# Moving three queries' additions, the output weights' loads and the first output pair's small work in a one-core decoder layer

## The chip, the cores and the metric

The kernel runs on one core of a Trainium2 chip. Its time is the device time of one execution in microseconds, taken as the median of several runs. All stages described below run on that core: TensorE (PE) multiplies, VectorE (DVE), ScalarE (ACT) and GpSimd (POOL) do the elementwise work, and transfers are issued by SyncE (SP) or by ACT, each on a queue of its own.

## What is computed

The input is `x` of 32 sequences of 64 tokens with 512 numbers each, that is 2048 tokens, all in float32. Three blocks follow each other, each added to its input:

```
x = x + attention(layernorm(x))      # 32 heads of 128, rmsnorm on q and k, softmax over 64 keys, @ Wo + bo
x = x + cross(layernorm(x), ctx)     # keys and values from a context of 64 x 128 per sequence, plus a skip product
x = x + experts(layernorm(x))        # softmax of 64 logits, top 8, weighted expert biases
```

Most of the arithmetic is in the first: q, k and v are products of 2048 x 512 by 512 x 4096 each, and the output is 2048 x 4096 by 4096 x 512.

## The kernel before

The tokens are 16 tiles of 128, and two halves of 8 tiles are worked one after the other. For each half a loop runs over 16 head groups of two heads (`hg`). A head group's q and k products are done by a fast matrix scheme with 7 products in place of 8, and from the second head group on by that scheme twice over: a `Window` holds both quads of tiles of the half (two units, t = 0 and 1) and computes 7 x 7 products. So there are 15 windows in each half, 30 in all.

A window's `project` has four outer stages, n = 0 to 3. Stage n hands `outer` two of the seven outer products, (1, 5), (2, 6), (7, 3), and in the last stage (4,) alone. `outer` stops several times (m = 0 to 3). PE's products go to three PSUM banks `pa`, `pb`, `pc`; `keep` (L670, or L673 on ACT) writes a bank into the `qk` tile with an addition, and `end` (L683) adds a bank to what is there. A bank that PE adds to again (`first=False`) waits until DVE has read it. In stage 3 the order is: product 1 in `pa`, product 2 in `pc`, their two reads, stop (3, 0); product 6 in `pa`, product 5 in `pb`, two reads, stop (3, 1); products 7 and 3, two reads, stop (3, 2); product 4, its read, stop (3, 3).

At each stop the work that `behind` names for (n, m) is issued first: `add` (L739) sums quarters of `qk` tiles on DVE for the second unit and on POOL for the first, and `squares` (L360) squares a tile on ACT for the rms norm. Then follow waiting operations and what `plan[n][m]` lists: a value product `v` (L391 on PE, L407 copies on ACT, L411 adds on DVE), the scaling of an earlier unit (`scale`: k on POOL L546 at once, q on DVE L548 at a later `take_waiting`), the turning of probabilities (`turn`: L253 on PE, L582 on ACT), and attention of an earlier unit (`attend`: scores L559, mixing L596, softmax L261 to L269). At the end of the window `sums_of_squares` (L792) multiplies the squares by ones on PE. Meanwhile POOL forms the next window's weight sums (L120, L152 to L155) into a buffer that SP's loads (L107) filled. In the last window of a half POOL has no such inner sums (L152 to L155) to form. `also(n, m, it)` adds a step to a stop.

The order on PE, DVE, ACT and POOL is the order of the program up to the end of the first output pair; SP's order is left to the planner of the language. An engine's stream is executed in order, and an instruction that waits holds what is behind it. This is true of the transfers that ACT and SP issue, too.

Before the last window `load_wo` (L823) loads the output weights: eight transfers of 1 MB in all, k for the head of a pair, n for the half of the columns. They reuse the two large buffers of the weights (`four_blocks`) and the seven blocks of the transposed input (`block`).

After the last window comes the output product. `first_out` works the first pair of tiles: seven products (1, 2, 3, 7, 6, 5, 4) of 16 matmuls, each cut in four chunks. `drain` steps through its 28 chunks with `go(count)`, and puts the last units' `scale`, `turn` and `attend` between them. After chunk number `done`, DVE does what `sums[done]` holds (L902: sums of the first pair's inputs) or the next of eight sums of output weights (`making_wo`, L874 and L882) at chunks 8, 10, 14, 15, 16, 18, 21, 22. Then `strassen_out` does the other seven pairs, while `advance` moves the tails (cross attention and experts) of finished tiles. Ahead of the tails a small product `wqk` of the cross attention's weights is made from `xw` (L1510 to L1536). The chunks of the second pair are drawn by `next(outs[1])`.

Of the kernel before, what the change touches and what calls it, by code (L numbers as in the profile page):

```python
# [41 lines left out]
def decoder_layer(  # L42
# [585 lines left out]
    class Window:  # L628
# [86 lines left out]
        def project(self, plan):  # L715

            units, hg = self.units, self.w.hg
            for unit in units:
                unit.qk_tiles()
            sq = self.sq = {}  # L720

            def of(places):
                return lambda t, j: units[t].all[:, places, j, :]

            def twice(place):
                return lambda t, j: (
                    units[t].all[:, place, j, :].unsqueeze(1).to_broadcast([P, 2, QT])
                )

            def squares(h, ab, t):  # L730
                sq[h, ab, t] = square(
                    units[t].qk[h, ab], f"{h}{ab}_{units[t].name}", ab
                )

            def add(t, j, to, what):

                to, what = (units[t].qk[it][:, j, :] for it in (to, what))
                on = nc.vector if t else nc.gpsimd
                on.tensor_tensor(to, to, what, ALU.add)  # L739


            behind = {
                (1, 3): lambda: [squares(0, 0, t) for t in range(2)],
                (2, 1): lambda: (
                    add(0, 0, (1, 0), (1, 1)),
                    add(0, 0, (1, 1), (0, 1)),
                ),
                (2, 2): lambda: (
                    add(0, 1, (1, 0), (1, 1)),
                    add(0, 1, (1, 1), (0, 1)),  # L750
                    add(1, 1, (1, 0), (1, 1)),
                ),
                (2, 3): lambda: (
                    add(1, 1, (1, 1), (0, 1)),
                    add(1, 0, (1, 0), (1, 1)),
                    squares(1, 0, 0),
                    squares(1, 1, 0),
                ),
                (3, 0): lambda: (
                    add(1, 0, (1, 1), (0, 1)),  # L760
                    squares(1, 0, 1),
                ),
                (3, 1): lambda: squares(1, 1, 1),
                (3, 2): lambda: squares(0, 1, 0),
                (3, 3): lambda: squares(0, 1, 1),
            }
            for n, args in enumerate(
                (
                    ((1, 5), of(slice(2, 4)), None, lambda j: bqd[:, j, bass.ts(hg, HG)]),
                    ((2, 6), of(slice(0, 3, 2)), twice(2)),  # L770
                    ((7, 3), of(slice(1, 3)), twice(2)),
                    ((4,), of(slice(1, 2)), of(slice(1, 2))),
                )
            ):

                banks = [self.bank(f"p{n}{i}") for i in range(3)]
                turned = [banks[(2 * n + i) % 3] for i in range(3)]
                for m, _ in enumerate(self.outer(args[0], turned, *args[1:])):
                    behind.get((n, m), lambda: None)()
                    take_waiting()  # L780
                    for it in plan[n][m]:
                        it()
# [31 lines left out]

    def load_wo(k, n, places):


        halves = []  # L820
        for i, it in enumerate(places):
            it = it.rearrange("p (g f) -> p g f", f=DH)
            nc.scalar.dma_start(  # L823
                out=it,
                in_=wo.rearrange("(g k p) f -> k p g f", k=HG, p=HD)[
                    k, :, i * KH : (i + 1) * KH, bass.ts(n, DH)
                ],
            )
            halves.append(it)
        return halves  # L830
# [63 lines left out]
    def first_out(a, right, s4, s1, done):  # L894


        (a11, a12), (a21, a22) = a
        xa, xb = load_x(0), load_x(1)
        la, ra, lb, rb_ = (xt[:, bass.ts(n, DH)] for xt in (xa, xb) for n in range(2))
        p1 = xpool.tile([P, D], F32, tag="x", name="p1_0")[:, 0:DH]  # L900
        def combine(op, to, x, y):
            return lambda: nc.vector.tensor_tensor(to, x, y, op)  # L902

        sums[3] = combine(ALU.add, s1, a21, a22)
        sums[4] = combine(ALU.subtract, a11, s1, a11)
        sums[5] = combine(ALU.subtract, s4, a12, a11)
        sums[7] = combine(ALU.subtract, a21, a22, a11)

        def product(i, it):
            py = out_block(f"{i}_0")  # L910
            yield from chunks(py, [(it, right[i])])
            return py

        def add(to, py):
            nc.vector.tensor_tensor(to, to, py, ALU.add)

        py = yield from product(1, a11)
        nc.scalar.copy(p1, py)
        yield
        py = yield from product(2, a12)  # L920
        add(la, py)
        nc.gpsimd.tensor_tensor(la, la, p1, ALU.add)
        yield
        py = yield from product(3, s4)
        add(ra, py)
        yield
        py = yield from product(7, a21)
        add(lb, py)
        add(rb_, py)
        yield  # L930
        py = yield from product(6, a11)
        add(p1, py)
        for to in (ra, lb, rb_):
            nc.gpsimd.tensor_tensor(to, to, p1, ALU.add)
        yield
        py = yield from product(5, s1)
        add(ra, py)
        add(rb_, py)
        add_bias(xa)
        done(0, xa)  # L940
        yield
        py = yield from product(4, a22)
        add(lb, py)
        add_bias(xb)
        done(1, xb)
# [396 lines left out]
    for n, (hg, half) in enumerate(groups):  # L1342
# [37 lines left out]
        else:  # L1380
# [34 lines left out]

            if n + 1 == len(groups):
                four = four_blocks("wo_0")
                wo_b = [[load_wo(k, 0, four[2 * k : 2 * k + 2])] for k in range(2)]
                a_0 = [[None, None], [None, None]]

                def mixture(t, h, place):
                    a_0[t][h] = load_mixed(t, h, place())

                def qk_buffer(name):
                    return work.tile([P, BLK], F32, tag="qk", name=name, bufs=4)

                also(2, 0, lambda: mixture(0, 1, lambda: block("a0_1")))
                also(2, 1, lambda: mixture(1, 0, lambda: block("a1_0")))
                also(2, 2, lambda: mixture(0, 0, lambda: block("a0_0")))
                also(2, 2, lambda: mixture(1, 1, lambda: qk_buffer("a1_1")))  # L1430
            double(Window(units, w, half), more)
    for k in (1, 0):
        wo_b[k].append(load_wo(k, 1, [block(f"wo{k}1{i}") for i in range(2)]))

# [25 lines left out]
    def drain():  # L1462
        done = 0

        def go(count):
            nonlocal done
            for _ in range(count):
                next(todo, None)
                done += 1
                take_waiting()  # L1470
                if done in sums:
                    sums[done]()
                elif done in (8, 10, 14, 15, 16, 18, 21, 22):
                    next(making_wo)

        go(3)
        line.turn()
        go(3)
        line.scale()
        go(3)  # L1480
        line.scale()
        go(3)
        line.attend()
        line.scale()
        go(4)
        line.scale()
        go(1)
        line.turn()
        go(2)
        line.attend()  # L1490
        go(4)
        line.turn()
        go(1)
        line.attend()
        a12 = load_mixed(2, 1, block("a12_1"))
        go(4)
        return a12
# [13 lines left out]
    for j, src in enumerate((xwq_t, xwk_t, xwv_t, xws_t)):  # L1511
        for b in range(2):
            half = slice(b * SEQ, (b + 1) * SEQ)
            (load if j < 2 else load_beside)(xw[half, j, half], src)
    rwt = work.tile([P, KC, NEXP], F32, tag="rwt", name="rwt", bufs=1)
    load_beside(rwt, rw_t.rearrange("(kc p) e -> p kc e", p=P))
    rb_b = work.tile([P, NEXP], F32, tag="rb", name="rb_b", bufs=1)
# [2 lines left out]
    eb_sb = work.tile([P, D], F32, tag="eb", name="eb_sb", bufs=1)  # L1520
    for half in range(2):
        load_beside(eb_sb[half * NEXP : (half + 1) * NEXP, :], eb)
    for n in range(6):
        next(outs[1])
        if n > 3:
            advance()

    pt = ps_t.tile([P, 2, P], F32, tag="pt", name="pt_xw")
    for j in range(2):
        nc.tensor.transpose(pt[:, j, :], xw[:, j, :], ident)  # L1530
    turned = work.tile([P, 2, P], F32, tag="kvs", name="turned")
    nc.scalar.copy(turned, pt)
    pw = ps_t.tile([P, P], F32, tag="pt", name="pt_wqk")
    nc.tensor.matmul(pw, turned[:, 1, :], turned[:, 0, :], start=True, stop=True)
    wqk = work.tile([P, P], F32, tag="wqk", name="wqk", bufs=1)
    nc.scalar.copy(wqk, pw)  # L1536
    for pair in range(1, NPAIR):
        for _ in outs.pop(pair, None) or strassen_out(pair, right, start_tail):
            advance()
# [53 lines left out]
```

## Time and profile before

| what | us |
|---|---|
| median of 3 runs | 1917.75 |
| lowest and highest of them | 1917.36 and 1920.27 |
| profiled execution, own time | 1920.47 |
| its span (first to last instruction) | 1918.7 |
| PE busy in the span | 1870.7 |
| DVE busy | 1256.2 |
| POOL busy | 1008.5 |
| ACT busy | 652.3 |

The granted TensorE clock was 0.99 in that execution. The windows of the first half lie between 56 and 683 us, those of the second half between about 738 and 1373 us; the first output pair runs from 1375 to 1439 us, and the remaining pairs and tails to the end. In the views, a line of a wait gives the waiting instruction, what released it, the total, the count and the longest. In a timeline a number in brackets is the idle time just before the instruction and what ended it. The record of a matmul of this kernel is half of a program's matmul, so that one of its products of 128 x 128 by 128 x 256 appears as two. PEld is the weight load of a matmul, which can run ahead of it.

### The profile page before, as it was taken

The page shows a single profiled execution, that of the slowest core. Times are in us where ns is not written, and L with a number is a line of the kernel's source. Part 1 is how long each engine was busy: PE and PEld are TensorE (multiplying, and loading weights), DVE is VectorE, ACT ScalarE, POOL GpSimd, SP SyncE. Part 2 cuts the span into 40 slices and gives each one's busy share as a digit, 9 for nine tenths or more (in the row PEclk, how much of TensorE's full clock was granted, in tenths as well). Part 3 has the DMA queues.
Part 4 walks back from the last instruction along what each step waited for, and adds up shares of the span by engine and source line. Part 5 has one row for each costly group of instructions (what it writes and reads, how often), then busy time and mean ns, then how long its engine had stood idle before and what let it go on. Part 6 is the DMA issues. An engine that isn't in the chain of part 4 may idle for free.

```text
span 1918.7 us, 40515 instructions
## 1 busy us (share of the span) xinstructions
PE 1870.7 (97%) x16838; PEld 1618.0 (84%) x16838; DVE 1256.2 (65%) x2107; ACT 652.3 (34%) x1573; POOL 1008.5 (53%) x859
## 2 busy tenths in 40 slices
PE   8999999999999999999999999999989999999996
PEld 7888888888888888888888888888877888888884
DVE  7867777776767759766667776666664545554544
ACT  2343444444333443444333444433312212221122
POOL 5856676665667549766677666565231121221120
PEclk9999999999999999999999999999999999999996
DMA  4244434334433343334433333443744231223100
GB/s 139 67 133 143 123 122 132 113 106 131 135 112 111 105 144 107 100 109 132 128 110 112 111 100 104 131 132 130 252 127 148 91 113 67 82 78 113 45 25 23
DMA packets 164648, 215.04 MB, mean 112 GB/s; under 512 B 10160, under 2 KB 135152, under 8 KB 160368
## 3 DMA queue, kind: packets, MB, share of 16 engines
q1 hardware_dynamic: 153808, 202.49, 32.5%
q10 hardware_dynamic: 10656, 9.96, 1.6%
q8 instruction: 132, 2.16, 0.5%
q14 instruction: 52, 0.43, 0.1%
HBM read 172.05 MB, written 40.37 MB: 111 GB/s over the span
## 4 chain that ended last, share of the span: by engine, by line
PE 84%; DVE 6%; POOL 4%; DMA 3%; issue 2%; ACT 1%; ACTq 0%; SPq 0%; POOLq 0%; DVEq 0%
PE p_w L659 30%; PE py L851 17%; PE va L391 10%; PE vb L391 7%; PE ms_w L792 3%; PE o L596 3%; PE s L559 3%; DVE qk L670 1%; PE pt_p L253 1%; PE pa L449 1%; PE py_x L1114 1%; PE e_x L1077 1%; DVE qk L739 1%; PE py_x L1112 1%; PE pl_f L1135 1%
## 5 line engine op out<-in xcount | busy, mean ns | idle before, releaser
L659 PE MATMUL p_w<-x,w 128*128 128x256 f32 x2940 | 724.7, 383 | 13.5 <-DVE qk L670 8.1
L659 PEld LDWEIGHTS p_w<-x,w 128*128 128x128 f32 x2940 | 521.7, 191 | 75.2 <-DVE qk L670 12.1
L391 PEld LDWEIGHTS va<-w,x 128*128 128x128 f32 x2048 | 268.8, 192 | 14.7 <-ACT v L407 1.8
L670 DVE TENSOR_TENSOR qk<-p_w,qk 128x512 f32<-128x512 f32 x360 | 212.4, 598 | 94.1 <-PE p_w L659 92.7
L391 PE MATMUL va<-w,x 128*128 128x128 f32 x2048 | 270.4, 275 | 1.4 <-ACT v L407 1.4
L683 DVE TENSOR_TENSOR qk<-p_w,qk 128x512 f32<-128x512 f32 x360 | 219.9, 620 | 60.2 <-PE p_w L659 56.2
L407 ACT COPY v<-va 128x256 f32<-128x256 f32 x256 | 95.5, 373 | 459.4 <-PE va L391 459.3
L120 POOL TENSOR_TENSOR w<-w 128x768 f32<-128x768 f32 x126 | 245.2, 1956 | 2.4
L269 POOL TENSOR_TENSOR prob<-prob,inv 128x512 f32<-128x512 f32 x64 | 77.6, 1212 | 319.9 <-DVE inv L268 316.6
L360 ACT ACTIVATE sq<-qk 128x512 f32<-128x512 f32 x256 | 161.0, 630 | 229.5 <-DVE qk L683 86.9
L546 POOL TENSOR_TENSOR qk<-qk,rs 128x512 f32<-128x512 f32 x128 | 173.1, 1352 | 102.8 <-DMA rs<-row_w 94.4
L851 PE MATMUL py<-wo,a 128*128 128x256 f32 x992 | 227.1, 382 | 0.0
L851 PEld LDWEIGHTS py<-wo,a 128*128 128x128 f32 x992 | 184.5, 190 | 33.1 <-issue 8.7
L391 PEld LDWEIGHTS vb<-w,x 128*128 128x128 f32 x1536 | 201.9, 192 | 9.8
L391 PE MATMUL vb<-w,x 128*128 128x128 f32 x1536 | 202.8, 275 | 0.0
L548 DVE SCALAR_TENSOR_TENSOR qk<-qk,gqk,rs 128x512 f32<-128x512 f32 x128 | 170.9, 1335 | 2.0 <-DMA rs<-row_w 1.3
L851 PE MATMUL py<-wo_t,a 128*128 128x256 f32 x672 | 156.4, 384 | 0.0
L851 PEld LDWEIGHTS py<-wo_t,a 128*128 128x128 f32 x672 | 124.9, 191 | 18.2 <-issue 1.6
L976 POOL TENSOR_TENSOR x<-x,p 128x256 f32<-128x256 f32 x42 | 42.8, 1038 | 174.5 <-ACT p L1029 77.5
L411 DVE TENSOR_TENSOR v<-vb,v 128x256 f32<-128x256 f32 x192 | 80.7, 420 | 53.4 <-PE vb L391 27.1
L739 POOL TENSOR_TENSOR qk<-qk 128x256 f32<-128x256 f32 x120 | 103.4, 863 | 10.5 <-DVE qk L683 5.8
L261 DVE TENSOR_REDUCE mx<-s 128x8 f32<-128x512 f32 x64 | 44.1, 689 | 94.5 <-PE s L559 94.4
(191 smaller groups left out, 2264.6 us busy)
## 6 DMA issues: line engine op xcount, KB each, us to landing
rs<-row_w SPq DMA_DIRECT2D x120, 512.0 KB
mixed<-ot SPq DMA_DIRECT2D x64, 512.0 KB
a<-mixed SPq DMA_DIRECT2D x32, 1024.0 KB
w<-in_wq_dram SPq DMA_DIRECT2D x64, 256.0 KB
w<-in_wk_dram SPq DMA_DIRECT2D x62, 256.0 KB
w<-in_wv_dram SPq DMA_DIRECT2D x62, 256.0 KB
wo<-in_wo_dram ACTq DMA_DIRECT2D x8, 1024.0 KB
x<-in_x_dram SPq DMA_DIRECT2D x20, 256.0 KB
```

Source lines behind the costliest of these rows:

```text
L120: on.tensor_tensor(*(it.rearrange("p c j d -> p (c j) d") for it in (out, a, b)), ALU.subtract)
L360: nc.scalar.activation(sq, of, AF.Square)
L391: nc.tensor.matmul(to[:, j, :], left[i][:, c, j, :], right[i][:, c, 2, :], start=first and j == 0 and c == 0, stop=c == 1, skip_group_chec ...
L407: nc.scalar.copy(self.v[h, ab], what)
L411: nc.vector.tensor_tensor(it, what, it, ALU.add)
L546: nc.gpsimd.tensor_tensor(k, k, rk, ALU.mult)
L548: lambda: nc.vector.scalar_tensor_tensor(q, q, gqk, rq, ALU.mult, ALU.mult)
L659: nc.tensor.matmul(bank[:, s, :], self.w.inner[o][i], inner_x[self.half, o][i], start=first and s == 0, stop=True, skip_group_check=True,)
L670: nc.vector.tensor_tensor(to(t, j), bank, add(t, j), ALU.add)
L683: nc.vector.tensor_tensor(to(t, j), bank, to(t, j), ALU.add)
L739: on.tensor_tensor(to, to, what, ALU.add)
L851: nc.tensor.matmul(py, a[:, g, :], b[g // KH][:, g % KH, :], start=n == 0 and g == 0, stop=n == last and g == NHG - 1,)
```

## The change

Four things are moved; the arithmetic is the same, apart from the engine of three additions.

1. In `project`, the second unit's sum `add(1, 0, (1, 0), (1, 1))` goes from stop (2, 3) to (3, 0), `add(1, 0, (1, 1), (0, 1))` and the square of (1, 0) from (3, 0) to (3, 1), and the square of (1, 1) from (3, 1) to (3, 2).
2. `load_wo` takes a queue. Of the eight transfers, those of k = 0 go to SP and those of k = 1 to ACT; the first two of k = 1 are issued at (1, 0) of the last window in place of before it, and its other two at (3, 1) in place of after it. The other two of k = 0 still come after it.
3. In the first output pair, the three additions of `p1` (L934) go from POOL behind chunk 20 to DVE behind chunk 23, and the second `scale` after the first `attend` comes two chunks earlier.
4. The four loads of `xw` that were on SP go to ACT's queue; the two transposes of `xw` come one chunk earlier, and one chunk is put between them and the product that uses them.

```diff
                 (2, 3): lambda: (
                     add(1, 1, (1, 1), (0, 1)),
-                    add(1, 0, (1, 0), (1, 1)),
                     squares(1, 0, 0),
                     squares(1, 1, 0),
                 ),
-                (3, 0): lambda: (
+                (3, 0): lambda: add(1, 0, (1, 0), (1, 1)),
+                (3, 1): lambda: (
                     add(1, 0, (1, 1), (0, 1)),
                     squares(1, 0, 1),
                 ),
-                (3, 1): lambda: squares(1, 1, 1),
-                (3, 2): lambda: squares(0, 1, 0),
+                (3, 2): lambda: (
+                    squares(1, 1, 1),
+                    squares(0, 1, 0),
+                ),
...
-    def load_wo(k, n, places):
+    def load_wo(k, n, places, queue):
...
-            nc.scalar.dma_start(
+            queue.dma_start(
...
+        sums[23] = lambda: [nc.vector.tensor_tensor(to, to, p1, ALU.add) for to in (ra, lb, rb_)]
...
         py = yield from product(6, a11)
         add(p1, py)
-        for to in (ra, lb, rb_):
-            nc.gpsimd.tensor_tensor(to, to, p1, ALU.add)
         yield
...
-                wo_b = [[load_wo(k, 0, four[2 * k : 2 * k + 2])] for k in range(2)]
+                wo_b = [[load_wo(0, 0, four[0:2], nc.sync)], []]
+                also(1, 0, lambda: wo_b[1].append(load_wo(1, 0, four[2:4], nc.scalar)))
...
+                also(
+                    3,
+                    1,
+                    lambda: wo_b[1].append(
+                        load_wo(1, 1, [block(f"wo11{i}") for i in range(2)], nc.scalar)
+                    ),
+                )
             double(Window(units, w, half), more)
-    for k in (1, 0):
-        wo_b[k].append(load_wo(k, 1, [block(f"wo{k}1{i}") for i in range(2)]))
+    wo_b[0].append(load_wo(0, 1, [block(f"wo01{i}") for i in range(2)], nc.sync))
...
         line.attend()
         line.scale()
-        go(4)
+        go(2)
         line.scale()
-        go(1)
+        go(3)
         line.turn()
...
-            (load if j < 2 else load_beside)(xw[half, j, half], src)
+            load_beside(xw[half, j, half], src)
...
-    for n in range(6):
+    for _ in range(5):
         next(outs[1])
-        if n > 3:
-            advance()
...
     nc.scalar.copy(turned, pt)
+    advance()
+    next(outs[1])
     pw = ps_t.tile([P, P], F32, tag="pt", name="pt_wqk")
     nc.tensor.matmul(pw, turned[:, 1, :], turned[:, 0, :], start=True, stop=True)
     wqk = work.tile([P, P], F32, tag="wqk", name="wqk", bufs=1)
     nc.scalar.copy(wqk, pw)
+    advance()
```

## The prediction

> **What bounds the kernel now.** I read the busy times first: PE is busy for 1870.7 of 1918.7 us, DVE as the next for 1256.2. So only PE's idle time is to be had, some 48 us, and what PE runs slowly. The second view is therefore PE's list of waits (waiter, releaser, total, count, longest):
>
> ```profile
> PE p_w L659 <- DVE qk L670: 8.1, 27, 0.9
> PE p_w L659 <- ACT qk L673: 3.6, 1, 3.6
> PE s L559 <- DVE qk L548: 2.9, 2, 2.3
> PE pt_p L253 <- POOL prob L269: 2.6, 1, 2.6
> PE pt_xw L1530 <- DMA xw<-in_xwq_t_dram: 2.3, 1, 2.3
> ```
>
> One short wait comes back in nearly every window; the others are single ones, all between the last window's start and the second output pair. I looked each up in the timeline (start, duration, engine, line). A steady window at stop (3, 0):
>
> ```profile
> 508.26 1.89 DVE L739 TENSOR_TENSOR qk<-qk 128x256 f32<-128x256 f32 x2
> 508.69 1.18 POOL L152 TENSOR_TENSOR w<-w 128x384 f32<-128x384 f32 x1
> 510.08 0.41 DVE L670 TENSOR_TENSOR qk<-p_w,qk 128x256 f32<-128x256 f32 x1
> 510.54 0.73 PEld L659 LDWEIGHTS p_w<-x,w 128*128 128x128 f32 x4 [0.47 <-DVE qk L670]
> 510.54 1.13 PE L659 MATMUL p_w<-x,w 128*128 128x256 f32 x4 [0.28 <-DVE qk L670]
> ...
> 1331.79 5.12 ACTq L823 DMA_DIRECT2D wo<-in_wo_dram x1
> 1336.95 0.84 ACT L673 ACTIVATE qk<-p_w,bqd 128x256 f32<-128x256 f32 x2 [6.55 <-issue]
> 1337.84 1.13 PE L659 MATMUL p_w<-x,w 128*128 128x256 f32 x4 [3.63 <-ACT qk L673]
> ...
> 1394.90 3.32 DVE L874 TENSOR_TENSOR wo<-wo,wo 128x2048 f32<-128x2048 f32 x1 [2.98 <-DMA wo<-in_wo_dram]
> 1399.03 0.92 PE L559 MATMUL s<-qk 128*64 128x64 f32 x24 [2.31 <-DVE qk L548]
> ...
> 1419.52 6.22 POOL L934 TENSOR_TENSOR x<-x,p 128x256 f32<-128x256 f32 x3 [10.29 <-DVE p L915]
> ...
> 1426.80 0.66 PE L253 MATMUL pt_p<-ident,prob 128*128 128x128 f32 x4 [2.64 <-POOL prob L269]
> ```
>
> DVE's two additions of (2, 3) end at 510.16, so the read of `pa` (L670) starts at 510.08 though its product was long there, and product 6, which adds to `pa`, waits. Next, the last window: ACT is held 5.12 us by the issue of one output weight transfer, and its read of a bank is behind that. Then DVE waits for output weights at L874, and q's scaling L548, which the scores need, is behind it. Last, POOL's three additions take 6.22 us beside DVE's weight sums and hold back the probabilities. The stretches (span, busy times, granted clock, DMA share, GB/s) show that three of these gaps cost twice:
>
> ```profile
> 1336.00:1344.00 8.00, 6.16 (x29) 5.59 (x30) 2.28 (x4) 2.31 (x6) 1.36 (x2) 0.79 1.09 380
> 1428.00:1432.00 4.00, 4.00 (x71) 3.02 (x70) 0.75 (x2) 0.18 (x2) 1.18 (x1) 0.57 0.63 247
> 1455.00:1459.00 4.00, 4.00 (x14) 3.40 (x13) 1.13 (x2) 0.52 (x2) 0.00 (x0) 0.57 0.96 401
> ```
>
> After each gap the clock dips: 8 x 0.21 = 1.68 us, 4 x 0.43 = 1.72 us and again 1.72 us of PE's time.
>
> **Part 1, the windows.** Start to start of L792, a window with the stall takes 599.24 to 641.28, that is 42.04 us; the next, in which POOL has no inner sums and DVE's two additions take 1.09 us, takes 641.28 to 682.79, 41.51. The stall is worth 0.53 us. PEld's list has 26 such waits (12.1 us), so 13.8 us is all there is.
>
> What takes its place? In the old times: the first addition ends at 508.94, products 1 and 2 are there by about 509.0 and 509.4 (two records of 0.22 us each from 508.35, and the 0.2 us that reads follow by), and the two reads end at 509.8. Product 6 wants `pa` at 510.10: no wait. Now the moved addition A, then L411 (0.34 from start to start), then the read of product 6 (0.41). Product 7 would want that bank at 510.10 + 0.87 + 0.89 = 511.86. L739 on DVE takes 0.41 to 1.22 us; the read ends at 510.9 or 511.8. It fits at both ends, barely at the upper. The second moved addition B starts at about 512.2 behind the other read; with 1.22 us the reads of products 7 and 3 end at 513.8 and 514.2, and product 4 wants its bank at 514.05. On ACT the square of (1, 1) now waits for B and stands before that of (0, 1), the turned probabilities' copy (0.59) and the last square; 0.95 us of idle time before L360 at 513.93 takes its 0.63. If B is late, the last square is up to 0.25 us later against L792, which already waits 0.2 us for it.
>
> Here a rule speaks against the move. The row is L739 on DVE, 407 to 1223 ns, long only where POOL's L152 runs. The Trainium skill, "SBUF — State Buffer", section "Who interferes with whom", says that a DVE instruction with two SBUF inputs and a GpSimd one that reads SBUF exclude each other, the second waiting for all of the first. POOL subtracts from 508.69 to 513.2 without a break, so by the rule A and B each stand before a lock of up to 1.1 us, and by the rule alone each costs about 1.5 us: the read would end at 512.1, a stall of 0.2 us. By the row nothing. I take 0.45 us won of 0.53 per window, between 0.28 and 0.53: 26 x 0.45 = **11.7 us** (7 to 14).
>
> **Part 2, the loads.** Four transfers of 1 MB stood together on ACT: 0.38, 0.59, 2.15, 5.12 us of issue. The last window takes 1323.50 to 1370.57 in the chain of waits, 47.07 against 41.51: 5.6 us, which is 3.63 of wait, 1.68 of clock and small rest. Now each queue gets two at a time; an issue on SP is not shown for this shape, so between 0.4 and 5.1 us, and I take 0.4 to 0.6, the first two on ACT. SP's two stand where a normal window's six weight loads do (L107, 1.5 MB, 0.42 to 0.47 us each), ahead of `row_w`, `rs` and `mixed`; in a normal window POOL waits 2.48 us for `rs` there and PE never. On ACT 1 us at (1, 0) holds a value copy, 1 us at (3, 1) the squares of this one window. Won: **5.3 us** (2 to 5.6).
>
> The rule against it: "DMA: Bandwidth & Descriptors", section "Issuing engines are not separate DMA queues", says that all transfers share the same engines and two queues save only the issue time, usually small. By that, 8 MB come no sooner and I would count 1 to 2 us. But the row shows issue time itself on the path: 5.12 us in one instruction.
>
> After the last window the four late transfers were issued from 1375.57 to 1383.9 and landed at 1394.88 (12.82 us in the chain). Now two go out at (3, 1), some 8 us sooner, beside the loads of `a`, which reach 426 GB/s by 1368 and are wanted from 1374.9; two on SP at about 1376. At the 340 to 390 GB/s of 1380 to 1396 they are there by about 1386. The first of them is read behind other DVE work at 1391.9, so the wait of 2.98 on DVE and the 2.31 on PE go: **2.3 us** (0 to 2.3). Behind them on SP, `rs` and two `x` loads come 3 to 6 us later than the queue alone would have them; they are wanted at 1392, with those 5 us to spare.
>
> **Part 3, the first pair.** Three additions of 0.42 us go to DVE behind chunk 23, where its weight sums (2.28 each) are past: 1.3 us of DVE in a stretch in which it then waited 5.16. POOL's L269 (1.04 alone, 2.90 beside a DVE sum at 1377.14) now starts at 1420.3 and ends by about 1423; the turn wants it at 1423.8. Gone: 2.64 and the dip of 1.72; I leave 0.4 for the shared port: **4.0 us** (1 to 4.4). The scale moved forward puts L548 before two weight sums in place of behind three: 0.62 at 1415.05 and 0.41 at 1408.15 go, **1.0 us** (-1 to 1), below nothing if a weight sum is then late for product 6.
>
> **Part 4, `xw`.** The four loads leave SP (2.99 us of issue), where they stood behind 2 MB of `a` (8.04 us from issue to landing), and go to ACT behind 1433.5, where ACT then idles 20.46 us. One chunk between covers ACT's 0.46. Gone: 2.27 + 0.46 + 1.72 = 4.45. But PE then comes about 5 us sooner to `ct` (issued at 1449.22) and to the `a` of its next products, whose loads ran at over 300 GB/s until 1451. I take **3.6 us** (0 to 4.5).
>
> **Sum.** 11.7 + 5.3 + 2.3 + 4.0 + 1.0 + 3.6 = 27.9 us. The profiled execution took 1920.47, 1.8 above its span and 2.7 above the median; the differences carry over: 1917.75 - 27.9 = 1889.9. With every term full, 31.5, it is 1886.
>
> **The rivals.** *The stall of the windows only moves* to product 7 or to L792: against it the row of 1.22, for it the 0.1 us that is left. Then 16.2 us remain: 1901.5. *The transfers stay the bound:* 8 MB come no sooner or displace `rs`, `x` and `a`, so that the single waits only change names; for it the 1.00 and more of DMA share from 1380 to 1396. Then 11.7 and some 2 us remain: 1904. *The change does not do what it says,* the same waits at other stops: 1917. *Slower, by the shared port:* an addition at (3, 0) loses to two POOL subtractions in a row. From A = 1.3 us on PE stalls at product 7, at 1.85 the windows are even, at 2.5 the kernel is (16.2 / 26 = 0.62 more). With 2.9 us, 26 x (1.6 - 0.53) = 28 lost against 16.2 won: 1930. Against it, none of 120 took more than 1.22.
>
> **How the numbers follow.** The forecast 0.65, windows unchanged 0.14, transfers 0.12, nothing 0.03, slower 0.06. About 0.2% (4 us) is what a measurement of this kernel can tell from no change; the first three are faster by more, 0.91. The range reaches from 1884, just under all terms full, over both middle rivals to 1906.
>
> **What would show it.** Windows of about 41.6 us from L792 to L792, and L659's waits for L670 gone; a last window within 1 us of that; no `ACTq` issue above 1 us there; L874 not waiting for a transfer; clock 1.00 in the three stretches. Wrong would be a new wait of product 7 or L792 in each window, or PE waiting for `a` or `ct` after 1440.

## The result and the profile after

The changed kernel takes 1888.5 us, the median of five runs from 1888.35 to 1890.42, against 1917.36 of before beside it (five runs, 1915.92 to 1920.27). The ratio is 0.9847, with a 95% interval of 0.9833 to 0.9861: 28.9 us less. The profiled execution took 1888.35 us, with a span of 1886.6. The spans of the two profiles differ by 32.1 us, more than the medians. At the end of the kernel the granted clock falls to 0.50, and not for equally long in each execution. Summed over stretches of 4 us of the whole execution, (1 - clock) x 4 is 18.7 us in the profile of before and 10.7 after; the last 35 us hold 13.6 and 9.1 of it, 5.1 of before's are the three dips that the prediction names, and 1.6 of after's lie at its start. So below, times are compared by the start of the same work in the two timelines, and only up to the second output pair.

PE was busy for 1870.7 us and is now for 1856.9. Of the 32.1 us of span, 18.3 are idle time of PE and 13.8 busy time. Part of that was work at a low clock, and part belongs to the windows' stall: it moved a window by 0.54 us, of which PE's list counts only 0.28 as idle. PE's list of waits (waiter, releaser, total, count, longest):

```profile
PE p_w L659 <- DVE qk L670: 2.9, 3, 1.2
...
PE kv L1067 <- DMA ct<-in_ctx_dram: 1.9, 1, 1.9
```

The 27 waits for L670, 8.1 us together, have become 3, of which one is 1.2. The waits for L673, L548, L269 and `xw`, the other four that the prediction set out from, are gone. New is one on the context `ct`. The prediction's lines leave out PE's longest single wait, 3.7 us for L1103 at the kernel's end; it is in both profiles. The steady window, stops (3, 0) and (3, 1), in the timeline (start, duration, engine, line):

```profile
503.98 0.41 DVE L739 TENSOR_TENSOR qk<-qk 128x256 f32<-128x256 f32 x1
504.02 1.24 POOL L153 TENSOR_TENSOR w<-w 128x384 f32<-128x384 f32 x1
...
505.11 0.75 DVE L670 TENSOR_TENSOR qk<-p_w,qk 128x256 f32<-128x256 f32 x2
505.33 0.99 POOL L154 TENSOR_TENSOR w<-w 128x384 f32<-128x384 f32 x1
...
505.77 0.84 DVE L739 TENSOR_TENSOR qk<-qk 128x256 f32<-128x256 f32 x1
...
505.92 1.03 PE L659 MATMUL p_w<-x,w 128*128 128x256 f32 x4
```

Addition A (503.98) starts 0.04 us ahead of POOL's subtraction L153 and takes 0.41. Of the two reads at 505.11 the first, of product 6, ends at about 505.5, and product 7, which adds to its bank, starts at 505.92 without a wait. B (505.77) takes 0.84, and PE does not wait for it. So it is in each of the 25 windows that had the stall: A 0.41 or 0.42 and 0.03 or 0.04 ahead of L153, B 0.84 or 0.85, and from L794 to L794 41.51 us where it was 42.05. The single places behind the windows, in the same timeline:

```profile
1308.20 1.01 SPq L824 DMA_DIRECT2D wo<-in_wo_dram  x2
...
1323.70 1.86 DVE L548 SCALAR_TENSOR_TENSOR qk<-qk,gqk,rs 128x512 f32<-128x512 f32 x1 [3.23 <-DMA rs<-row_w]
...
1325.13 1.02 ACTq L824 DMA_DIRECT2D wo<-in_wo_dram  x2
...
1326.21 1.99 PE L659 MATMUL p_w<-x,w 128*128 128x256 f32 x8 [1.21 <-DVE qk L670]
...
1348.56 2.35 ACTq L824 DMA_DIRECT2D wo<-in_wo_dram  x2
...
1353.16 1.06 PE L794 MATMUL ms_w<-sq,ones 128*32 128x256 f32 x12 [0.38 <-ACT sq L360]
...
1398.79 2.89 POOL L269 TENSOR_TENSOR prob<-prob,inv 128x512 f32<-128x512 f32 x1 [11.00 <-DVE inv L268]
...
1401.76 0.62 PE L253 MATMUL pt_p<-ident,prob 128*128 128x128 f32 x4
...
1428.43 0.46 PE L1067 MATMUL kv<-ct,wqk 128*128 128x128 f32 x2 [1.87 <-DMA ct<-in_ctx_dram]
```

And two stretches (span, busy times of PE, PEld, DVE, ACT and POOL, granted clock, DMA share, GB/s) of the places in which PE was at 0.57 before:

```profile
1400.00:1404.00 4.00, 4.00 (x21) 3.17 (x20) 4.00 (x3) 0.59 (x1) 1.67 (x1) 1.00 0.91 250
1428.00:1432.00 4.00, 3.57 (x21) 3.29 (x22) 2.53 (x2) 0.74 (x2) 1.26 (x1) 1.00 1.01 420
```

The starts of the same work on PE, before and after, give the sum by place:

| start of | before | after | total gained | gained in this stretch | forecast |
|---|---|---|---|---|---|
| L792/L794 ahead of the last window | 1323.43 | 1308.10 | 15.3 | 15.3 | 11.7 |
| L792/L794 behind it | 1370.50 | 1351.08 | 19.4 | 4.1 | 5.3 |
| first output block | 1374.91 | 1356.32 | 18.6 | -0.8 | in the 5.3 |
| product 7 | 1400.97 | 1379.85 | 21.1 | 2.5 | 2.3 |
| product 5 | 1418.82 | 1396.58 | 22.2 | 1.1 | 1.0 |
| product 4 | 1431.79 | 1405.13 | 26.7 | 4.4 | 4.0 |
| second pair's product 1 | 1458.43 | 1428.95 | 29.5 | 2.8 | 3.6 |

The same program was profiled a second time (below). There the stretches gain 16.6, 5.6, -1.5, 2.5, 1.1, 4.4 and 4.4, in sum 33.1: the last window, what follows it, and the last row differ from one execution to the next.

### The profile page after: what moved, and what is told of

It is laid out like the page before. It is cut to its first block, busy times and chain, and to the rows that moved or that the text cites. A ratio compares the mean times of both kernels' runs of the same rounds, so it can differ in the third digit from the quotient of the medians.

```text
span 1886.6 us, 40521 instructions
## 1 busy us (share of the span) xinstructions
PE 1856.9 (98%) x16838; PEld 1613.8 (86%) x16838; DVE 1259.9 (67%) x2110; ACT 653.0 (35%) x1573; POOL 1014.8 (54%) x856
## 4 chain that ended last, share of the span: by engine, by line
PE 88%; DVE 5%; DMA 3%; POOL 2%; issue 1%; ACT 1%; ACTq 0%; SPq 0%; POOLq 0%; DVEq 0%
PE p_w L659 32%; PE py L852 17%; PE va L391 11%; PE vb L391 8%; PE ms_w L794 3%; PE o L596 3%; PE s L559 3%; PE pt_p L253 1%; PE pa L449 1%; PE e_x L1077 1%; PE py_x L1114 1%; PE py_x L1112 1%; PE pl_f L1135 1%; PE pt_x L253 1%; DMA rs<-row_w 1%
## 5 line engine op out<-in xcount | busy, mean ns | idle before, releaser
L670 DVE TENSOR_TENSOR qk<-p_w,qk 128x512 f32<-128x512 f32 x360 | 213.1, 599 | 87.4 <-PE p_w L659 84.5
L407 ACT COPY v<-va 128x256 f32<-128x256 f32 x256 | 96.2, 376 | 495.8 <-PE va L391 495.6
L269 POOL TENSOR_TENSOR prob<-prob,inv 128x512 f32<-128x512 f32 x64 | 79.0, 1235 | 300.7 <-DVE inv L268 297.5
L546 POOL TENSOR_TENSOR qk<-qk,rs 128x512 f32<-128x512 f32 x128 | 177.8, 1390 | 105.9 <-DMA rs<-row_w 91.2
L852 PEld LDWEIGHTS py<-wo,a 128*128 128x128 f32 x992 | 184.3, 190 | 33.1 <-issue 8.7
L548 DVE SCALAR_TENSOR_TENSOR qk<-qk,gqk,rs 128x512 f32<-128x512 f32 x128 | 181.6, 1419 | 4.2 <-DMA rs<-row_w 3.9
L411 DVE TENSOR_TENSOR v<-vb,v 128x256 f32<-128x256 f32 x192 | 80.8, 421 | 55.8 <-ACT v L407 28.6
L739 POOL TENSOR_TENSOR qk<-qk 128x256 f32<-128x256 f32 x120 | 102.8, 857 | 10.5 <-DVE qk L683 5.8
```

What stands on the lines that cost most here:

```text
L407: nc.scalar.copy(self.v[h, ab], what)
L411: nc.vector.tensor_tensor(it, what, it, ALU.add)
L546: nc.gpsimd.tensor_tensor(k, k, rk, ALU.mult)
L548: lambda: nc.vector.scalar_tensor_tensor(q, q, gqk, rq, ALU.mult, ALU.mult)
L670: nc.vector.tensor_tensor(to(t, j), bank, add(t, j), ALU.add)
L852: nc.tensor.matmul(py, a[:, g, :], b[g // KH][:, g % KH, :], start=n == 0 and g == 0, stop=n == last and g == NHG - 1,)
```

## The experiments

The theory was that the four parts each take away the waits named for them, with little in common. The rivals: the windows' stall only moves; the shared port makes the additions long; the loads only exchange their waits. The first four kernels do one part each on the kernel before, the others alter the changed kernel. Before was 1918.24 us beside the first four (43 runs from 1913.36 to 1921.94), 1918.26 beside the next four and 1920.18 beside the last two (7 runs each).

### Part 1 alone

The diff is that of `behind` in part 1, on the kernel before.

> The kernel before with part 1 alone (the second unit's two additions and two squares moved). Theory: every one of the 26 stalled windows loses its 0.53 us and nothing comes in its place, so 13 to 15 us are won: about 1903. L792 to L792 is 41.5 us in all windows. Rival: part of the windows' gain needs the rest of the change, or a new wait takes half of it: 7 us or less, 1910 or more, with a window above 41.7.

Measured: 1903.8 us (4 runs), ratio 0.9933 (0.9916 to 0.9949), 14.4 us less. From the third window of the first half and the second one of the other half on, the windows take 41.51, except for one of 42.33 and the last one, which has the loads' wait still (46.92). So the stall is won in full and does not move. L673, L269 and L548 wait as they did before (3.5, 2.6 and 2.4), and `xw` 1.2 in place of 2.3.

### Part 2 alone

```diff
-                wo_b = [[load_wo(k, 0, four[2 * k : 2 * k + 2])] for k in range(2)]
+                wo_b = [[load_wo(0, 0, four[0:2], nc.sync)], []]
+                also(1, 0, lambda: wo_b[1].append(load_wo(1, 0, four[2:4], nc.scalar)))
...
-        wo_b[k].append(load_wo(k, 1, [block(f"wo{k}1{i}") for i in range(2)]))
+    wo_b[0].append(load_wo(0, 1, [block(f"wo01{i}") for i in range(2)], nc.sync))
```

> The kernel before with part 2 alone (output weights on two queues, two of them earlier). Theory: the last window falls from 47.07 to about 43 us, the scores no longer wait 2.3 us behind L874, and some 6 to 7 us are won: about 1911. Rival (two queues bring nothing sooner): only the issue time on ACT is won, 4 us, 1913.5, with L874 still waiting for a transfer.

Measured: 1908.72 us (8 runs), ratio 0.9958 (0.9943 to 0.9973), 9.5 us less by the medians and about 8 by the ratio. The last window took 41.51, so its whole 5.56 is won there. PE's waits that are left say why it is more than expected:

```profile
PE pt_p L253 <- POOL prob L269: 2.6, 1, 2.6
...
PE s L559 <- DVE qk L548: 0.6, 1, 0.6
...
PE pt_xw L1536 <- DMA xw<-in_xwq_t_dram: 0.4, 1, 0.4
```

The wait for L269 is untouched. The 2.3 us for q's scaling (L548) are gone, as meant; the 0.6 left is the other, shorter wait of before, which part 3 is for. But the wait for `xw`, which belongs to part 4, is down from 2.3 to 0.4, and the granted clock behind it, from 1448 to 1460, is 1.00. Parts 2 and 4 overlap by some 2 us and, in this profile, by the low clock behind them. Why `xw` is there sooner was not tried by itself. Nor does part 2 alone tell its two means apart, the second queue and the later places.

### Part 3 alone

```diff
+        sums[23] = lambda: [nc.vector.tensor_tensor(to, to, p1, ALU.add) for to in (ra, lb, rb_)]
...
-        for to in (ra, lb, rb_):
-            nc.gpsimd.tensor_tensor(to, to, p1, ALU.add)
...
-        go(4)
+        go(2)
         line.scale()
-        go(1)
+        go(3)
```

> The kernel before with part 3 alone (three additions on DVE behind chunk 23, the second scale two chunks earlier). Theory: the turn's wait of 2.64 and the clock dip of 1.72 behind it go, and the 1.0 of the scores' wait: 5 us, about 1912.5, with a granted clock of 1.00 in the stretch after that turn. Rival: with the loads still late DVE is behind, the moved scale only changes which operation waits, and the additions on DVE cost what they save: under 2 us, 1915.5 or more.

Measured: 1915.23 us (20 runs), ratio 0.998 (0.9971 to 0.999): 3.0 us less by the medians, 3.8 by the ratio. The wait of 2.64 for L269 is gone. Stretches of this kernel, with the granted clock third from the end:

```profile
1424.00:1428.00 4.00, 4.00 (x79) 3.32 (x78) 2.74 (x8) 1.57 (x4) 1.35 (x2) 1.00 0.82 278
...
1448.00:1452.00 4.00, 4.00 (x15) 3.29 (x14) 0.37 (x2) 0.27 (x1) 0.00 (x0) 0.57 0.97 408
```

The first one, where PE ran at 0.57 before, is at 1.00. The second, behind the wait for `xw` (1.8 in this kernel), is at 0.57, as it was. So what part 3 names did go. In this profile the second pair's product 1 starts at 1451.89, 6.5 us sooner than before, so up to there the 5 expected are won. The measured gain is below them, and what lies behind that point differs by as much between runs of one kernel (these 20 reach from 1906.86 to 1919.06).

### Part 4 alone

```diff
-            (load if j < 2 else load_beside)(xw[half, j, half], src)
+            load_beside(xw[half, j, half], src)
```

with the moved chunks of part 4.

> The kernel before with part 4 alone (xw's four loads on ACT, one chunk between its transposes and the product). Theory: the wait of 2.27 + 0.46 and the dip of 1.72 go, less a wait of up to 2 us for ct, as in the changed kernel: 2.5 to 4.5 us, about 1914. Rival: PE waits for ct or a instead by the same amount: within 1 us of 1917.4.

Measured: 1915.53 us (20 runs), ratio 0.9988 (0.998 to 0.9997): 2.7 us less by the medians, 2.3 by the ratio. There is no wait for `xw` and none for `ct`, and the second pair's product 1 starts at 1454.45 in place of 1458.43.

By the medians the four alone add up to 14.4 + 9.5 + 3.0 + 2.7 = 29.6 us, by the ratios to about 27; together they give 28.9. The profiles show an overlap that these sums hide in the spread of the ends. At the start of the second pair's product 1 the four kernels are 15.1, 11.0, 6.5 and 4.0 us ahead of before, 36.6 in sum, and the changed kernel 29.5 or 33.1. Some 3.4 of part 2's lie behind product 4, where part 4 works, and 1.2 of part 3's before product 7, where part 2 works.

### Both additions at (3, 0)

```diff
-                (3, 0): lambda: add(1, 0, (1, 0), (1, 1)),
-                (3, 1): lambda: (
-                    add(1, 0, (1, 1), (0, 1)),
-                    squares(1, 0, 1),
-                ),
+                (3, 0): lambda: (
+                    add(1, 0, (1, 0), (1, 1)),
+                    add(1, 0, (1, 1), (0, 1)),
+                ),
+                (3, 1): lambda: squares(1, 0, 1),
```

> The changed kernel with the second moved addition, B, at (3, 0) right behind A, in place of (3, 1). In the trace of the changed kernel A runs at 503.98, and DVE then idles 0.37 us for a copy on ACT, while POOL's L153 runs from 504.02 to 505.26. Theory (B is held until POOL's subtraction ends): the read of product 6 ends at about 506.2 in place of 505.5, product 7 wants its bank at 505.92, so some 0.3 us per window are lost, 26 x 0.3 = 8: about 1896, with L659 waiting for L670 in each window. Rival (B takes its 0.41 us in the idle time): within 2 us of 1888.5.

Measured: 1900.36 us (4 runs), ratio 0.9906 (0.9891 to 0.9921), 11.9 us more than the changed kernel. PE waits for L670 28 times again, 7.0 us together, and a window takes 41.95. The timeline of the same stop:

```profile
508.33 1.57 DVE L739 TENSOR_TENSOR qk<-qk 128x256 f32<-128x256 f32 x2
508.36 1.25 POOL L153 TENSOR_TENSOR w<-w 128x384 f32<-128x384 f32 x1
...
510.15 0.74 DVE L670 TENSOR_TENSOR qk<-p_w,qk 128x256 f32<-128x256 f32 x2
...
510.61 1.13 PE L659 MATMUL p_w<-x,w 128*128 128x256 f32 x4 [0.18 <-DVE qk L670]
```

The two additions take 1.57 us beside POOL's 1.25: A 0.41 as before, and B 1.12, since it ends 0.29 us behind POOL's instruction. B ends at 509.90, an addition of values (L411, 0.41) is next, the read of product 6 starts at 510.15, and product 7, which adds to the bank that it reads, waits. The rival's "within 2 us" is refuted: it matters that B stands behind the reads. 25 windows of 0.44 are 11.0 us of the 11.9 (11.3 by the ratios).

### SP's first two transfers at (1, 2)

```diff
-                wo_b = [[load_wo(0, 0, four[0:2], nc.sync)], []]
+                wo_b = [[], []]
+                also(1, 2, lambda: wo_b[0].append(load_wo(0, 0, four[0:2], nc.sync)))
```

> The changed kernel with SP's first two output weight loads at (1, 2) of the last window in place of before it, so that they stand behind that window's rs loads on SP. Theory: the row's write and rs's read no longer queue behind 2 MB; DVE does not wait 3.23 us for rs at L548, and PE's 1.21 us for L670 go: 1 to 1.5 us, about 1887, last window 41.5 to 42 us. Rival (rs is late for another reason): last window stays at 43 us, or the loads now delay those of a and PE waits behind the window.

Measured: 1889.24 us (4 runs from 1887.68 to 1894.47), ratio 0.9853 (0.9833 to 0.9873). This edit did not do what it was meant to: SP's order is the planner's, and it put the two transfers at the same place of SP's stream, ahead of `row_w`. So the run is a second look at the changed kernel. As such it tells something: the last window took 41.51 in place of 42.98, and PE did not wait for L670 there, since `rs` landed 5.4 us after its issue in place of 7.3.

### No transfer on ACT at (3, 1)

Beside the edit above, the other two of k = 1 go to SP:

```diff
-                        load_wo(1, 1, [block(f"wo11{i}") for i in range(2)], nc.scalar)
+                        load_wo(1, 1, [block(f"wo11{i}") for i in range(2)], nc.sync)
```

> As the last one, and the two loads at (3, 1) go to SP, so that ACT's issue of 2.35 us does not stand before the squares. Theory: L794's waits for L360 in the last window (0.86 + 0.50 against the usual 0.24) go, 0.8 us: about 1886. Rival: SP issues them after the loads of a, and L875 waits for a transfer again: 1888 or more.

Measured: 1887.14 us (4 runs, 1886.28 to 1891.01), ratio 0.9842 (0.9825 to 0.9858). L794 no longer waits for the last squares: from its start to the first output block are 4.41 us, as before the change (5.24 with it). In this profile `rs` took 7.6 us again, and the last window 43.08. The time does not differ from the changed kernel's by more than runs do. SP now has four transfers from the window's last 6 us on, each issued in 0.4 us, and PE does not wait for the last units' `rs`.

### The context on ACT's queue

```diff
-        nc.sync.dma_start(out=ct, in_=ctx_flat[bass.ts(t, P), :])
+        (nc.scalar if t < 2 else nc.sync).dma_start(out=ct, in_=ctx_flat[bass.ts(t, P), :])
```

on top of the two edits above.

> As the last one, and the ct loads of the first two tiles go to ACT's queue, past the loads of a on SP. Theory: PE's wait of 1.87 us for ct at L1067 goes: about 1884.5, the fastest of all. Rival: it lands no sooner, since the transfer engines are full there (share 1.06 at 1424 to 1428), or PE waits for a next: 1886.

Measured: 1889.67 us (4 runs), ratio 0.9856 (0.9837 to 0.9874). The wait for `ct` is 0.53 in place of 1.87, and the second pair's product 1 starts at 1425.85, 3.1 us sooner than in the changed kernel's profile above. But with `ct` on SP the second profile of that kernel (below) has it at 1425.29, so the 3.1 are not the edit's. The execution as a whole is not faster; 15.8 us went to low clock in it, against 10.7.

### The changed kernel again, and one with no output weights ahead of `rs`

The second kernel gives SP no output weights before the last window's `rs`:

```diff
-                wo_b = [[load_wo(0, 0, four[0:2], nc.sync)], []]
-                also(1, 0, lambda: wo_b[1].append(load_wo(1, 0, four[2:4], nc.scalar)))
+                wo_b = [[], []]
+                also(1, 0, lambda: wo_b[0].append(load_wo(0, 0, four[0:2], nc.scalar)))
+                also(1, 3, lambda: wo_b[1].append(load_wo(1, 0, four[2:4], nc.scalar)))
...
-                        load_wo(1, 1, [block(f"wo11{i}") for i in range(2)], nc.scalar)
+                        load_wo(1, 1, [block(f"wo11{i}") for i in range(2)], nc.sync)
```

> The changed kernel itself, unaltered, for its own spread and for a second profile of its last window beside the other kernel of this call. Both theories: 1888.5 within 1.5 us in the median. If rs is late by chance of the execution, this profile's last window may take 41.5 us in place of 42.98, with rs landing 5.1 to 5.5 us after its issue; if the lateness belongs to the kernel, 43.0 again, with 7.3.

> The changed kernel, but SP takes no output weights before the last window's reciprocals: wo00's two transfers go to ACT at (1, 0), wo10's two to ACT at (1, 3), wo11's to SP behind the window. In six profiles with wo00's 2 MB ahead of them on SP, the reciprocals' copies (rs) landed 5.1 to 5.5 us after POOL was free for them in four (last window 41.5 us) and 7.3 to 7.4 in two (43.0). Theory: those 2 MB are what makes rs late. Then POOL's wait for rs is about 4.2 us here, as in a normal window, DVE's L548 does not stand before the read L670, the last window takes 41.5 us and the squares' wait before the first output block (0.8) is gone: 1.5 to 2.3 us less than the changed kernel in a profile of the long kind, about 1886.5 to 1888. Rival: rs is late in some executions whatever stands ahead of it, by mixed's transfer beside it; then a wait of 5 to 7 us is seen here too and the time is that of the changed kernel, 1888.5 to 1889.

Measured: the changed kernel 1887.07 us (4 runs, 1885.46 to 1890.43), ratio 0.9835 (0.9813 to 0.9857); the other 1891.03 (4 runs, 1889.87 to 1894.34), ratio 0.9859 (0.9833 to 0.9885). First the changed kernel's second profile:

```profile
1320.25 1.87 DVE L548 SCALAR_TENSOR_TENSOR qk<-qk,gqk,rs 128x512 f32<-128x512 f32 x1 [1.01 <-DMA rs<-row_w]
...
1345.86 3.02 ACTq L824 DMA_DIRECT2D wo<-in_wo_dram  x2
...
1424.77 0.46 PE L1067 MATMUL kv<-ct,wqk 128*128 128x128 f32 x2 [0.26 <-DMA ct<-in_ctx_dram]
```

DVE got `rs` after 1.01 us where it waited 3.23, PE does not wait for L670, and the last window takes 41.51. ACT's issue at (3, 1) is 3.02 where it was 2.35, and from L794 to the first output block it takes 5.92. The wait for `ct` is 0.26 in place of 1.87. So the same program has both waits in one execution and next to none of them in another, and its medians are 1.4 us apart. Now the kernel without loads ahead of `rs`:

```profile
1315.76 0.32 SPq L537 DMA_DIRECT2D rs<-row_w  x1
...
1319.61 1.27 POOL L546 TENSOR_TENSOR qk<-qk,rs 128x512 f32<-128x512 f32 x1 [0.97 <-DMA rs<-row_w]
...
1345.80 10.42 SPq L824 DMA_DIRECT2D wo<-in_wo_dram  x3
...
1372.16 1.27 POOL L546 TENSOR_TENSOR qk<-qk,rs 128x512 f32<-128x512 f32 x1 [10.78 <-DMA rs<-row_w]
...
1381.01 0.92 PE L559 MATMUL s<-qk 128*64 128x64 f32 x24 [2.85 <-POOL qk L546]
```

Here `rs` is issued at 1315.76 and POOL can start at 1319.61, 3.9 us later. With the 2 MB ahead of it, seven profiles show 5.0 to 5.9 us (five of them) and 7.3 to 7.6 (two). So `rs` comes 1 to 4 us sooner without these loads, as the theory had it. But the planner, with the loads gone, also put the first `rs` ahead of `mixed`, as it stands in other windows; what share is the loads' own and what is that of `mixed` is not told apart. The kernel before, and the three that keep its loads, have the first `rs` ahead of `mixed` and no output weights ahead of it on SP, but four of them on ACT's queue: there it took 5.9 to 6.0. So the loads need not stand ahead of `rs` on its own queue to make it late. Of the seven only the two of the long kind made PE wait. The theory's time was wrong: three of the four transfers left on SP hold it from 1345.80 to 1356.22, 10.42 us, and the last units' `row_w` and `rs` stand behind them. POOL waits 10.78 us, its scaling of k (L546) is late, and the scores wait 2.85. The wait of 1.2 was exchanged for one of 2.85. In the two experiments before, SP has the same three transfers ahead of `row_w`, and each took 0.4 us of issue. Here the four ahead of them came later, two on ACT at (1, 0) and two at (1, 3); that this is what holds SP was not tried by itself.

## Why the prediction was right, point by point

The forecast was 1889.9, and 1888.5 is within its range and 1.4 us below. Its likeliest case happened. Four of its six terms are within 0.8 us of the table. The other two err in opposite directions: the windows were 3.6 us too low, and the last window with what follows it (4.1 - 0.8 = 3.3 against 5.3) 2.0 too high. So the sum, 29.5 against 27.9, is better than its parts; that the two cancel is luck. Not all of the signs that the prediction named came: the last window took 42.98 and not within 1 us of 41.6, one issue on ACT took 1.94 us, and PE did wait for `ct`, which it had called a sign of being wrong.

**The windows: right, and hedged too far.** The prediction took 0.45 us won per window, between 0.28 and 0.53, for a possible wait of product 7. The windows went from 42.05 to 41.51, all of the stall: 25 of them are 13.5 us. Another 1.3 came in the first half's second window, from 41.73 to 40.41, and the first windows of the halves make up the rest of the 15.3. These 1.8 us the prediction did not name. In that second window PE waited 1.4 us for a value copy on ACT (L407), and it does not after. But part 2 alone and part 4 alone have no such wait there, and their window took 42.09 and 41.42, with 1.6 and 1.3 us of waits for L670; with part 1 it takes 40.1 to 40.9 (41.4 in the fifth experiment). So it goes with part 1, and by which wait stays open. The stall also was not the 26 times 0.53 of the text but 25 times 0.54. The rival with its stall moved to product 7 did not occur in the changed kernel, but the fifth experiment shows it real: with B one stop sooner it is there in each window.

**The rule on the port and the row: no contradiction.** The rule of the Trainium skill ("SBUF — State Buffer", "Who interferes with whom") makes the shared port a lock, and the order of issue decides who waits. The prediction took POOL to be first both times, and set the row, 0.41 to 1.22, against that. But the row is the rule at work. In the profile after, 63 of DVE's 120 additions (L739) took over 0.5 us: each started while an instruction of POOL was under way and ended 0.28 us behind the end of that. The other 57 took 0.41 or 0.42. So B ends at 506.61 and L154 at 506.33, in the fifth experiment B at 509.90 and L153 at 509.61, and in before the second addition at 510.15 and L152 at 509.87. The prediction's "long only where L152 runs" holds for the 1.22 alone; 35 others started beside POOL's own L739 and took up to 0.95.

So what decides is when POOL's instruction ends. That A finds none under way, by 0.03 or 0.04 us, no line of before shows, and the prediction did not argue it: that is luck. Behind L153, A would have taken about the 1.5 us that the prediction worked out for "the rule alone"; in the fifth experiment A and B together take 1.57, and 0.44 of the 0.54 are lost. Nor does the order of two such starts always tell who is held: in the last window L548 starts at 1323.70, 0.04 ahead of POOL's L546 (1323.74), takes 1.86 where 0.74 is usual, and ends 0.56 behind it. DVE was busy with its 120 additions of L739 for 72.8 us after and 80.4 before, so the new places are also the cheaper ones.

**The last window's loads: right in kind, 5.3 against 3.3 after what the squares gave back.** ACT's transfer of 5.12 and the wait for L673 are gone. Two claims were too light. "SP's two stand where a normal window's six weight loads do, PE never waits": in the profile `rs` landed 7.3 us after its issue, L548 (1.86) came late on DVE, and the read L670 behind it held PE for 1.21. In a second profile of the same program `rs` took 5.0 and PE did not wait, so it is a risk of the execution, not a fixed cost (the window and what follows it gain 4.1 there, since the squares lost 1.5); the run with neither the loads nor `mixed` ahead of `rs` measured 3.9. And "on ACT 1 us at (3, 1)" was 2.35 (1.70 to 3.02 in the others). The loads of `a` precede it on SP; that they are the cause was not tried. It put the last squares behind, and L794 and with it the first output block lost 0.8. With those transfers on SP that loss was nil in two experiments.

The rule of the Trainium skill that two queues save only the time of issue ("DMA: Bandwidth & Descriptors", "Issuing engines are not separate DMA queues") would have given 1 to 2 us. The trace has 4.1 in that window, or 5.5 where `rs` is in time, for the reason the prediction gave: the time of issue was itself 5.12. It is not ACT's alone: in the last experiment three such transfers held SP for 10.42 us.

**The loads behind the window: right.** L874, now L875, waits for no transfer, and product 7 is 2.5 us better against 2.3. That `rs` and `x` behind SP's two transfers have time to spare held, and in two experiments for four transfers too; it did not where three of them held SP for 10.42 us.

**The first pair: right, 4.4 and 1.1 against 4.0 and 1.0.** POOL's L269 took 2.89 us, beside DVE's weight sums, near the 2.7 that the prediction's times leave it. It ended at 1401.68, and PE's turn of the probabilities followed at 1401.76, with no wait. So the three additions were what was in the way; but the cover is a few hundredths of a microsecond wide, where the prediction had 0.8 us. The clock there is 1.00.

**`xw`: right in kind, 2.8 against 3.6.** Its 0.85 of allowance for `ct` was not quite enough: PE waited 1.87 for `ct` in the profile, the wait that the prediction had named as what would speak against it, and 0.26 in the second profile of the same program, where the stretch gains 4.4. Part of what the term claims also goes with part 2 alone, so its place in the sum is a matter of order.

**The other rivals.** That the transfers stay the bound is refuted by part 2 alone, with 8 to 9.5 us. The one with slower windows by the port needed 1.3 us for A to begin; the longest of DVE's 120 additions was 1.01 after, and A was 0.41.

**The low clock behind the gaps: right, but not by the gaps' length.** The prediction counted 1.7 us for each of three dips, and all three went. The trace records a dip as 3.41 us at 0.50, or a multiple of that, and within one execution the dips start whole multiples of 3.41 us apart: those of before, at 1339.25, 1427.99 and 1455.30, are 26 and 8 apart. In periods of this grid (span, busy times of PE, PEld, DVE, ACT and POOL, granted clock, DMA share, GB/s), before:

```profile
1397.27:1400.68 3.41, 1.65 (x76) 1.61 (x80) 3.41 (x3) 0.00 (x0) 0.00 (x0) 1.00 0.20 76
...
1424.58:1427.99 3.41, 1.20 (x8) 1.12 (x9) 0.58 (x1) 0.45 (x1) 2.16 (x2) 1.00 0.32 97
1427.99:1431.40 3.41, 3.41 (x54) 2.49 (x56) 0.75 (x2) 0.14 (x1) 0.58 (x1) 0.50 0.74 290
```

and after:

```profile
1425.39:1428.80 3.41, 1.54 (x9) 1.09 (x8) 0.00 (x0) 0.00 (x0) 0.63 (x1) 1.00 1.07 346
```

PE was idle for 2.21 us of the period from 1424.58, and the next is at half clock. The scores' wait of 2.31 before falls into two periods, 1.76 of it into the one from 1397.27, and no dip follows; nor does one behind the 1.87 for `ct`. In the twelve profiles, from 110 to 1845 us, each of the twelve periods with 1.9 us or more of idle PE was followed by a dip; of the ten with 1.3 to 1.9 one was, and one dip more, with part 4 alone at 1516.42, came behind 0.8. So whether a gap costs twice depends on where it falls in the grid, and the grid lies differently in each profile: in the same wait for L548 that left before's clock at 1.00, part 1 alone (2.4 us) and part 4 alone (2.7) met a dip.

None of the variants is faster than the changed kernel by more than the spread of their runs.

## What to carry to other kernels

When a bank is read by an engine that has other work in its stream, put that work behind the read that PE waits for next, and look for what the moved work then meets: here one stop for one addition decided between the whole gain and a fifth of it. Count a large transfer's issue as time on the engine that issues it, and look at what small transfers stand behind it on its queue. When single waits of PE are removed, look for low clock behind each, which can cost as much again, and for the next wait in the line, here `ct`, before the gain is booked. And when two engines share a port, look at when the other's instructions end: that, more than a mean time, says what an addition costs at a place.

## What was not expected of the hardware

- With two transfers of 1 MB ahead of it on SP's queue, `rs` (512 KB) landed in 5.0 to 5.9 us or in 7.3 to 7.6, in runs of one order of SP's stream there; with neither these nor `mixed` ahead, in 3.9; with four such transfers on ACT's queue and none ahead on SP, in 5.9 to 6.0. In the long kind both first halves of `rs` were there at once (POOL's two L546 followed each other without a break), in the short one they came apart. What decides between the two is open.
- The same two transfers of 1 MB took 1.01 to 1.15 us of ACT's time at (1, 0) and 1.70 to 3.02 at (3, 1), behind the loads of `a`. Three on SP took 0.4 us each in two kernels and 10.42 together in a third.
- The low clock behind PE's single gaps went with the gaps. It comes in pieces of 3.41 us, and PE's idle time in the piece before foretells it better than a gap's length: with part 3 alone it came behind waits of 1.8 and 0.5, which fall into one period (2.3 us of idle PE), and not behind the 2.85 of the last experiment, which falls into two (1.1 and 1.8). What decides between 1.8 and 1.9, where the record has both, is open. The low clock at the kernel's end did not go. It differs from one execution to the next by several us, as much as the runs of one kernel do.
- An addition on DVE that started while POOL's instruction was under way ended 0.28 us behind it in 63 cases of 63, with 256 numbers in a row, and L548, with 512, ended 0.56 behind it.
